# Expert tiles of 128 slots, two to a round, and another schedule for the last batch

## The chip, the cores and the metric

One core of a Trainium2 chip runs the whole program. The time is the device time of one execution in microseconds; what is compared is the median of several executions. The core's engines are TensorE (PE, with its weight loads listed as PEld), VectorE (DVE), ScalarE (ACT), GpSimd (POOL) and SyncE (SP), which issues nearly all transfers. Everything is in float32.

## The reference

The input is eight images of 256 channels and 32 x 32 pixels, so 1024 tokens of 256 numbers each. Two layers follow one another.

Layer 0 is a deformable attention: from a group norm of x come queries and sampling offsets; 64 keys and values per group are sampled; the scores get a bias that a small network of three layers computes for each pair of a pixel and a sampled point.

Layer 1 works on tokens:

```python
t = _to_tokens(x)
t = t + _L1_attn_ref(_ln_t(t), L1_attn_q_weight)   # sigmoid((t q) t^T) t
t = t + _L1_ffn_ref(_ln_t(t), L1_ffn_router_w, L1_ffn_w1, L1_ffn_b1, L1_ffn_w2, L1_ffn_b2)

# in _L1_ffn_ref: 8 experts, the best 2 for each token
probs = softmax(tokens @ router_w.T)
rw, re = top_k(probs, 2);  rw = rw / max(rw.sum(-1, keepdims=True), 1e-12)
combine = zeros((N, 8)).at[arange(N)[:, None], re].set(rw)
out = tokens
for e in range(8):
    h = gelu(tokens @ w1[e] + b1[e], approximate=False)
    out = out + combine[:, e:e + 1] * (h @ w2[e] + b2[e])
```

Each token needs two of the eight experts only, so a batch (one image) has 2048 pairs of a token and an expert.

## The kernel before

The eight batches run one behind another, and several stages of different batches are interleaved by Python generators, so that the order written in the program is the order on each engine's queue. A batch has 64 turns. Each turn does two of the 128 steps of the bias network: `first_layer` (L444: on POOL or DVE), `rectify` (ACT), `second_layer` (L462: matmuls `h2p`, then ACT or DVE), and every second turn `third_layer` (L480: matmuls `sim`). These matmuls are there in every turn. At every eighth turn `terms` (L413) loads two tables (`ta`, `nb`), which are used from three turns later on. Beside this a turn advances:

- `side`: the preparation of the next batch (`prep`, L227) and the softmax of this one;
- `mains`: the layer-1 attention. `attention` (L585) makes two generators. `upper` runs from turn 53 of a batch. `rest` begins at turn 0 of the next batch and goes on for some 55 turns: the last softmax, `to_query` (matmuls `wp`, `bp`, `q`), `slots` (twelve slots of matmuls `ap`, a sigmoid, matmuls `vp`), `finish` (layer norm, `un`, logits `lq`), then `route`, then 16 scatters;
- `mixtures`: the experts (`experts`, L867), one step where `mix` (L1038) says that one is due;
- `sums`: `combine` (L937), which gathers the results of a token's two experts (16 gathers on POOL), weighs and adds them and writes the output, one of 22 steps a turn.

`route` (L780) picks two experts for each token, counts the tokens of each expert, and gives every pair a slot. Slots are arranged in tiles that belong to one expert each. A tile has 256 slots; in the worst case 15 tiles are needed, and 15 are always computed. Row counts per expert are compared with the multiples of 256 in a constant of 8 x 8 x 4 numbers, from which come the first tile of each expert (`ends`), each pair's row (`slot`) and the expert of each tile (`expert`). POOL scatters the tokens to these rows of `xs` in device memory, with 16 indirect transfers of 128 rows.

`experts` is a pipeline of three stages over the tiles. In iteration n it multiplies tile n-2 by its second weight (`yp`, four matmuls), adds the bias on DVE (`yt`, L901) and writes `ys`; it issues the rows `xl` of tile n+2 and both weights of tile n+1, the latter behind one register load that fetches the expert's number; it multiplies tile n-1 by its first weight (`hp`, four matmuls of 256 columns) with a gelu on ACT (`ht`, L922); and it transposes tile n (`tp`, then the copy `xg`). Weight tiles have three buffers each. That is 19 steps: two that only load, and n from 0 to 16.

```python
        if of == b - 2 and b < NB - 1:
            due = i in (24, 26) or i > 26 and i % 2 and i not in (35, 37, 39, 61, 63)
        elif of == b - 3:
            due = i in (3, 7, 9)
```

So the experts of batch b-2 stand in 16 turns of batch b, and their last three steps in batch b+1. In batch 7 the second form of the rule holds: batch 5's experts follow batch 4's in turns above 9 that are odd or divisible by three, and batch 6's get turns 62 and 63. What is left stands behind the last turn, in a loop over `rest` of batch 7 (L1105): a step at every second advance outside the attention, and at every advance from the routing on. When the scatters of batch 7 have been issued, its experts run alone, interleaved with batch 6's `combine`, and then batch 7's `combine`.

SyncE works its queue in order: a transfer that waits for its data holds up those behind it.

Of the kernel before, what the change touches and what calls it, by code (L numbers as in the profile page):

```python
# [9 lines left out]
F32 = mybir.dt.float32  # L10
I32 = mybir.dt.int32
AF = mybir.ActivationFunctionType
ALU = mybir.AluOpType
# [14 lines left out]
SLOTS = 256  # L28
TILES = (2 * N + E * (SLOTS - 1)) // SLOTS
# [9 lines left out]
    ("ident", 128), ("gavg", 128), ("base", 512), ("basef", 128),  # L39
    ("gq", 1), ("cx", 1), ("cy", 8), ("rev", 64),  # L40
    ("ones", 128), ("before", 128), ("full", 256), ("tiles", (E - 1) * TILES), ("form", 12),
# [53 lines left out]
def tile_conv_attn_hybrid(ctx: ExitStack, tc: tile.TileContext, x, par, qw, w1, w2_, cst, out):  # L95
# [9 lines left out]
    wpool = ctx.enter_context(tc.tile_pool(name="w", bufs=3))  # L105
# [105 lines left out]
    xss = [nc.dram_tensor(f"xs{n}", [TILES * SLOTS, C], F32, kind="Internal").ap() for n in range(2)]  # L211
# [15 lines left out]
    def prep(b, xb, st):  # L227
# [41 lines left out]
        for t in range(KS * KS):  # L269
# [9 lines left out]
        oa = one.tile([P, 2, NJ], F32, name="oa")  # L279
        nc.scalar.activation(  # L280
            oa.rearrange("p k (y x) -> p k y x", x=8), oc.rearrange("p (y k) x -> p k y x", k=2), AF.Gelu
        )
# [4 lines left out]
        for g in range(2):  # L287
            for c in range(2):
                nc.tensor.matmul(
                    op.rearrange("p (c k g j) -> p c k g j", c=2, k=2, g=2)[:, c, :, g, :],  # L290
                    lhsT=pw[:, 2 * g + c : 2 * g + c + 1].to_broadcast([P, P]), rhs=oa, start=True, stop=True,
                )
        opf = psum("opf")
        nc.tensor.matmul(
            opf[:, 0:128].rearrange("p (k j) -> p k j", k=2),
# [6 lines left out]
        nc.vector.scalar_tensor_tensor(gk[:, 0:512], gk[:, 0:512], 4.0, base, ALU.mult, ALU.add)  # L302
# [7 lines left out]
        fl = one.tile([P, 2 * NJ], F32, name="fl")  # L310
# [9 lines left out]
        fr = one.tile([P, 2, 64], F32, name="fr")  # L320
# [22 lines left out]
        hx = one.tile([P, 256], F32, name="hx")  # L343
# [238 lines left out]
    def attention(b, st, o, rt):  # L582
# [152 lines left out]
        def rest():  # L735
# [10 lines left out]
            for n, _ in enumerate(slots([(q, mp) for q in range(4) for mp in range(2 if q < 2 else 0, 4)], True)):  # L746
                if n % 3 == 0:
                    yield
                    others()
# [7 lines left out]
            yield from route(lqs, rt)  # L757
# [3 lines left out]
            for n in range(16):  # L761
# [9 lines left out]
                yield  # L771
# [8 lines left out]
    def route(lqs, rt):  # L780
# [6 lines left out]
        revv = rev.rearrange("p (m e) -> p m e", e=E)  # L787
# [14 lines left out]
        def pick(name):  # L802
# [28 lines left out]
        nc.tensor.matmul(cnt, lhsT=cst_("ones"), rhs=sums, start=False, stop=True, skip_group_check=True)  # L831
        need = one.tile([P, E, E, 4], F32, name="need")
        nc.vector.tensor_tensor(
            need, cnt[:, 8, :].unsqueeze(1).unsqueeze(3).to_broadcast([P, E, E, 4]),
            cst_("full").rearrange("p (e f n) -> p e f n", e=E, f=E), ALU.is_gt,
        )
        nc.vector.tensor_reduce(ends[:, 1:9], need.rearrange("p e f n -> p e (f n)"), AX.X, ALU.add)
        for c in range(2):
# [4 lines left out]
            at, ends[:, 0:8].unsqueeze(1).to_broadcast([P, 8, E]), float(SLOTS), cnt[:, 0:8, :], ALU.mult, ALU.add  # L843
        )
        place = one.tile([P, 2, 8], F32, name="place")
        for c, oh in enumerate((oh1, oh2)):
# [5 lines left out]
        which = one.tile([P, TILES, E - 1], F32, name="which")  # L852
        nc.vector.tensor_tensor(
            which, ends[:, 1:8].unsqueeze(1).to_broadcast([P, TILES, E - 1]),
            cst_("tiles").rearrange("p (t e) -> p t e", e=E - 1), ALU.is_le,
# [11 lines left out]
    def experts(b, rt):  # L867
        xs = rt["xs"]
        yv = dram.tile([TILES * SLOTS, C], F32, name="ys")
        tiles = {}  # L870

        def fetch(t):
            xl = low("xl")
            nc.sync.dma_start(out=xl, in_=xs[t * SLOTS : (t + 1) * SLOTS, :].rearrange("(s p) c -> p s c", p=P))  # L874
            tiles[t] = [None, None, xl]

        def weights(t):
            e = nc.sync.value_load(rt["expert"][0:1, t : t + 1], min_val=0, max_val=E - 1)
            f1 = wpool.tile([P, 2 * C + 2], F32, name="w1")
            nc.sync.dma_start(out=f1, in_=w1[bass.ds(e, 1)].rearrange("e p c -> (e p) c"))  # L880
            f2 = wpool.tile([P, 3 * C], F32, name="w2")
# [347 lines left out]
```

## Time and profile before

| | us |
|---|---|
| time, median of 3 runs | 3216.83 (3212.77 to 3220.61) |
| the profiled execution | 3218.55, of which 3216.8 is the span of its instructions |
| before the first turn | 72.9 |
| turns of batch 0, 1, 2 | 277.9, 337.4, 367.6 |
| turns of batches 3 to 6 | 376.0, 378.9, 375.1, 379.2 |
| turns 0 to 62 of batch 7 | 392.4 |
| last turn and last `rest` up to the end of its queries | 46.4 |
| last attention | 44.6 |
| end of the attention, routing | 30.1 |
| last scatters, up to the first rows of batch 7's experts | 31.4 |
| batch 7's experts | 75.1 |
| batch 7's sums | 31.8 |

A turn is told in the trace by its first `h2p` matmul: each turn has 16 records of them (the trace shows two records for each float32 matmul). Within a run of matmuls the time from one start to the next is the price; the listed durations overlap. Times are in microseconds from the first instruction.

### The profile page before, as it was taken

The page shows a single profiled execution, that of the slowest core. Times are in us where ns is not written, and L with a number is a line of the kernel's source. Part 1 is how long each engine was busy: PE and PEld are TensorE (multiplying, and loading weights), DVE is VectorE, ACT ScalarE, POOL GpSimd, SP SyncE. Part 2 cuts the span into 40 slices and gives each one's busy share as a digit, 9 for nine tenths or more (in the row PEclk, how much of TensorE's full clock was granted, in tenths as well). Part 3 has the DMA queues.
Part 4 walks back from the last instruction along what each step waited for, and adds up shares of the span by engine and source line. Part 5 has one row for each costly group of instructions (what it writes and reads, how often), then busy time and mean ns, then how long its engine had stood idle before and what let it go on. Part 6 is the DMA issues. An engine that isn't in the chain of part 4 may idle for free. (4 is left out here: it accounts for less than half of the span.)

```text
span 3216.8 us, 50328 instructions
## 1 busy us (share of the span) xinstructions
PE 2928.8 (91%) x19468; PEld 1465.1 (46%) x19468; DVE 2173.7 (68%) x2996; ACT 1841.1 (57%) x2435; POOL 1547.5 (48%) x945
## 2 busy tenths in 40 slices
PE   3888998899999998999989999999999999988986
PEld 2223343334545454554535445354544546523765
DVE  4898678967785787756876587757777464586122
ACT  3666565656566556655566566655566566545322
POOL 2546344744464454634555365543646343364123
PEclk7999999999999999999999999999999999999998
DMA  3311101210344123432335224441234333532277
GB/s 100 89 32 45 21 19 27 69 29 19 85 122 129 32 65 98 136 91 50 87 88 145 55 61 103 117 133 33 66 90 141 81 84 97 147 96 64 66 248 235
DMA packets 421567, 281.20 MB, mean 87 GB/s; under 512 B 283088, under 2 KB 378064, under 8 KB 421328
## 3 DMA queue, kind: packets, MB, share of 16 engines
q1 hardware_dynamic: 408752, 242.80, 28.4%
q0 software_dynamic: 12288, 33.57, 3.4%
q8 instruction: 153, 2.51, 0.3%
q10 hardware_dynamic: 288, 1.62, 0.1%
q14 instruction: 86, 0.70, 0.1%
HBM read 204.51 MB, written 73.40 MB: 86 GB/s over the span
## 5 line engine op out<-in xcount | busy, mean ns | idle before, releaser
L453 POOL TENSOR_TENSOR h<-ta,nb 128x1024 f32<-128x1024 f32 x512 | 1060.7, 2073 | 1122.9 <-PE h2p L466 1052.8
L466 PE MATMUL h2p<-h,pr__97 64*64 64x512 f32 x8192 | 1026.8, 611 | 118.8 <-DVE h L474 86.8
L474 DVE TENSOR_TENSOR h<-h2p,nc 128x1024 f32<-128x1024 f32 x512 | 624.2, 1219 | 518.0 <-PE h2p L466 512.4
L472 ACT ACTIVATE h<-h2p,pr__97 128x1024 f32<-128x1024 f32 x512 | 569.7, 1113 | 516.0 <-PE h2p L466 514.9
L451 DVE TENSOR_TENSOR h<-ta,nb 128x1024 f32<-128x1024 f32 x512 | 765.3, 1495 | 0.7 <-ACT ta L427 0.5
L458 ACT ACTIVATE h<-h 128x1024 f32<-128x1024 f32 x512 | 536.8, 1049 | 82.8 <-POOL h L453 82.7
L466 PEld LDWEIGHTS h2p<-h,pr__97 64*64 64x64 f32 x8192 | 256.1, 133 | 639.9 <-issue 303.6
L493 PE MATMUL sim<-h,pr__97 128*32 128x512 f32 x4096 | 506.5, 613 | 0.0
L493 PEld LDWEIGHTS sim<-h,pr__97 128*32 128x32 f32 x4096 | 108.6, 111 | 375.4 <-issue 375.4
L896 PE MATMUL yp<-w,ht 128*128 128x256 f32 x960 | 241.8, 396 | 18.7 <-ACT tn L630 10.7
L701 PE MATMUL ap<-qt,tn 128*128 128x256 f32 x1024 | 250.5, 388 | 0.5 <-ACT nc L439 0.5
L715 PE MATMUL vp<-tt,sg 128*128 128x256 f32 x1024 | 243.3, 381 | 0.3 <-ACT sg L706 0.3
L922 ACT ACTIVATE ht<-hp,w 128x256 f32<-128x256 f32 x240 | 100.8, 471 | 239.9 <-PE hp L916 200.6
L916 PE MATMUL hp<-xg,w 128*128 128x256 f32 x960 | 229.4, 382 | 6.0 <-ACT gk L299 2.8
L965 POOL DMA_INDIRECT gs<-ys,slot x128 | 139.1, 1087 | 193.2 <-DMA ys<-yt 57.8
L701 PEld LDWEIGHTS ap<-qt,tn 128*128 128x128 f32 x1024 | 185.2, 190 | 88.5 <-issue 55.9
L896 PEld LDWEIGHTS yp<-w,ht 128*128 128x128 f32 x960 | 178.8, 195 | 85.1 <-issue 31.8
L715 PEld LDWEIGHTS vp<-tt,sg 128*128 128x128 f32 x1024 | 193.2, 190 | 33.2 <-issue 6.9
L901 DVE TENSOR_TENSOR yt<-yp,w 128x512 f32<-128x512 f32 x120 | 82.6, 688 | 176.6 <-PE yp L896 137.9
L916 PEld LDWEIGHTS hp<-xg,w 128*128 128x128 f32 x960 | 183.0, 191 | 33.3 <-ACT gk L299 3.7
L763 POOL DMA_INDIRECT xs<-ut,slot x128 | 166.9, 1304 | 47.9 <-DVE slot L850 26.2
L276 DVE SCALAR_TENSOR_TENSOR oc<-qp,pr__97,oc 128x128 f32<-128x128 f32 x280 | 168.7, 603 | 7.2
(264 smaller groups left out, 2550.6 us busy)
## 6 DMA issues: line engine op xcount, KB each, us to landing
w<-in_w SPq DMA_DIRECT2D x120, 384.0 KB, 3.9
ta<-fd SPq DMA_DIRECT2D x128, 256.0 KB, 5.5
w<-in_w SPq DMA_DIRECT2D x120, 257.0 KB, 3.2
xl<-xs SPq DMA_DIRECT2D x120, 256.0 KB, 3.0
ys<-yt SPq DMA_DIRECT2D x120, 256.0 KB, 2.3
nb<-fd SPq DMA_DIRECT2D x128, 128.0 KB, 5.2
xb<-in_x SPq DMA_DIRECT2D x8, 1024.0 KB, 7.9
x<-in_x SPq DMA_DIRECT2D x8, 1024.0 KB, 8.5
```

Of the source, the lines that this page charges most:

```text
L276: nc.vector.scalar_tensor_tensor(oc, tap, dw[:, t : t + 1], oc, ALU.mult, ALU.add)
L451: nc.vector.tensor_tensor(h1, a, b, ALU.max)
L453: nc.gpsimd.tensor_tensor(h1, a, b, ALU.subtract)
L458: nc.scalar.activation(h1, h1, AF.Relu)
L466: nc.tensor.matmul(h2p[gs, r, :], lhsT=par_("w2")[rs, gs], rhs=h1[rs, g].rearrange("p y x -> p (y x)"), start=True, stop=True, tile_positi ...
L472: nc.scalar.activation(h2, h2p, AF.Relu, bias=par_("cb2"))
L474: nc.vector.tensor_tensor(h2.rearrange("p r (y x) -> p r y x", x=W), h2p.rearrange("p r (y x) -> p r y x", x=W), nc_.unsqueeze(3).to_broad ...
L493: nc.tensor.matmul(sim[32 * q : 32 * q + 32, :], lhsT=par_("z3")[:, 15 - m : 47 - m], rhs=h2s[2 * u + q // 2][:, q % 2, :], start=False, s ...
L701: nc.tensor.matmul(ap[:, u, :], lhsT=tn[:, k, m0 : m0 + P], rhs=qt[:, k, quarter(q)], start=(k == 0), stop=(k == 1),)
L715: nc.tensor.matmul(vp[:, i, :], lhsT=sg_[:, u, i * P : (i + 1) * P], rhs=tt[:, 2 * mp + u, :], start=(first and u == 0 and i == 0), stop=( ...
L896: nc.tensor.matmul(yp[:, s, :], lhsT=ht[:, f, s * P : (s + 1) * P], rhs=f2[:, f * C : (f + 1) * C], start=(f == 0), stop=(f == 1),)
L916: nc.tensor.matmul(hp[:, f, :], lhsT=f1[:, k * C + f * P : k * C + (f + 1) * P], rhs=xg[:, k, :], start=(k == 0), stop=(k == 1),)
```

## The change

- Batches 0 to 6 have tiles of 128 slots. At most 23 are needed (24 with a spare), and two neighbouring tiles, which may belong to different experts, form a round. 12 rounds are always computed, each of 256 rows. Batch 7 keeps 15 tiles of 256.
- A round loads `xl` and writes `ys` as before. It loads two first and two second weights, each behind a register load of its own. `hp` has eight matmuls of 128 columns, gelu four calls; `yp`, `yt`, `tp` keep their shapes. An expert stage has 16 steps.
- The two weights have pools of their own with two buffers each, every buffer for two tiles. The second weight of round n is now loaded in iteration n (it is used in n+2), the first weight of round n+1 also in iteration n but behind that iteration's gelu. In batch 7's experts these places change too.
- `route` takes the tile size, counts the tiles of each expert first and sums them up in a second step; three small tiles now lie in PSUM.
- `prep` shares buffers (`oa`, `fl`, `fr`, `hx` lie in others), and one addition is split in two; constants shrink from 1599 to 767 columns.
- `mix`: in batches 2 to 6 the steps at turn 59 and at turns 3 and 7 of the next batch are gone. In batch 7 batch 4 has its last step in turn 1, batch 5 its 16 in turns 2 to 11, 24 to 26, 33, 35, 37 and 39, and batch 6 its first eight in the odd turns from 45 to 59.
- In batch 6's `rest`, which runs in batch 7's turns, the attention takes a slot in each turn (13 advances instead of 18), and two scatters go in a turn.
- Behind the last turn, a step of batch 6's experts stands at every fourth advance outside the attention instead of at every second; from the routing on at every advance, as before.

```diff
-                if n % 3 == 0:
+                if n % 3 == 0 and b != NB - 2:
                     yield
                     others()
...
-                yield
+                if n % 2 or b != NB - 2:
+                    yield
...
+        slots_ = LARGE if b == NB - 1 else SMALL
+        several = LARGE // slots_
+        rounds = -(-tiles_of(slots_) // several)
...
+        def weights(t, pool, width, w, name):
+            f = pool.tile([P, 2, width], F32, name=name)
+            for u in range(several):
+                n = t * several + u
+                e = nc.sync.value_load(rt["expert"][0:1, n : n + 1], min_val=0, max_val=E - 1)
+                nc.sync.dma_start(out=f[:, u, :], in_=w[bass.ds(e, 1)].rearrange("e p c -> (e p) c"))
+            return f
...
+            if n + 2 < rounds:
                 fetch(n + 2)
-            if n + 1 < TILES:
-                weights(n + 1)
+            if n < rounds:
+                second[n] = weights(n, w2pool, 3 * C, w2_, "w2")
...
                 for f in range(2):
-                    for k in range(2):
-                        nc.tensor.matmul(
-                            hp[:, f, :], lhsT=f1[:, k * C + f * P : k * C + (f + 1) * P], rhs=xg[:, k, :],
-                            start=(k == 0), stop=(k == 1),
-                        )
+                    for u in range(several):
+                        us = slice(u * slots_, (u + 1) * slots_)
+                        for k in range(2):
+                            nc.tensor.matmul(
+                                hp[:, f, us], lhsT=f1[:, u, k * C + f * P : k * C + (f + 1) * P], rhs=xg[:, k, us],
+                                start=(k == 0), stop=(k == 1),
+                            )
...
+            if n + 1 < rounds:
+                first[n + 1] = weights(n + 1, w1pool, 2 * C + 2, w1, "w1")
...
-        if of == b - 2 and b < NB - 1:
-            due = i in (24, 26) or i > 26 and i % 2 and i not in (35, 37, 39, 61, 63)
-        elif of == b - 3:
-            due = i in (3, 7, 9)
+        if b == NB - 1:
+            due = i in {
+                b - 3: (1,), b - 2: (2, 3, 4, 6, 7, 8, 9, 10, 11, 24, 25, 26, 33, 35, 37, 39),
+                b - 1: range(45, 60, 2),
+            }.get(of, ())
+        elif of == b - 2:
+            due = i in (24, 26) or i > 26 and i % 2 and i not in (35, 37, 39, 59, 61, 63)
         else:
-            due = b == NB - 1 and (i >= TURNS - 2 if of == b - 1 else of < b and i > 9 and (i % 2 or i % 3 == 0))
+            due = of == b - 3 and i == 9
...
-        if sorted_ or not attending and n % 2:
+        if sorted_ or not attending and n % 4 == 3:
             step(mixtures)
```

## The prediction

> **What bounds the kernel now.** I read the busy shares first, then the busy time by stage, with the 64 turns of a batch told apart by the starts of the second-layer matmuls (16 records a turn).
>
> ```profile
> PE 2928.8 (91%) x19468; PEld 1465.1 (46%) x19468; DVE 2173.7 (68%) x2996; ACT 1841.1 (57%) x2435; POOL 1547.5 (48%) x945
> ```
>
> PE is the likely bound, but a share is a mean; the stages say where. In the next fence the columns are the window, its length, each engine's busy time, the granted clock, the DMA share and GB/s. The rows: batch 1 (no expert work in its turns), batch 2 (16 steps of it), batch 3 (19, as in batches 4 to 6), batch 7 without its last turn; then, after the turns, the end of the last attention with the routing, the last scatters, the last batch's experts.
>
> ```profile
> 350.80:688.20 337.40, 304.15 (x2122) 127.15 (x2121) 264.28 (x342) 200.86 (x250) 181.70 (x101) 0.97 0.16 35
> 688.20:1055.80 367.60, 350.63 (x2375) 171.58 (x2374) 258.36 (x354) 223.92 (x294) 176.95 (x101) 0.99 0.29 79
> 1055.80:1431.80 376.00, 358.64 (x2434) 181.88 (x2433) 272.38 (x373) 229.30 (x304) 193.86 (x117) 1.00 0.35 90
> 2565.00:2957.40 392.40, 359.81 (x2377) 178.99 (x2377) 252.12 (x322) 229.64 (x289) 188.43 (x125) 0.98 0.36 98
> ...
> 3048.40:3078.50 30.10, 24.83 (x114) 18.93 (x113) 11.27 (x39) 8.71 (x18) 2.17 (x3) 0.94 0.54 173
> 3078.50:3109.90 31.40, 27.35 (x130) 22.13 (x129) 5.56 (x10) 8.74 (x20) 15.45 (x16) 1.00 0.77 257
> 3109.90:3185.00 75.10, 67.55 (x313) 55.43 (x313) 15.26 (x29) 21.37 (x48) 15.47 (x16) 0.93 0.88 289
> ```
>
> Batch 2 adds 46 us of PE work to batch 1 and only 30 us of time: a step of expert work partly fills turns in which PE waits. So a removed step isn't worth its PE time; it is worth what its turn is longer than the same turn without it. Batches 1 and 2 give that directly. Turns 59 and 60 of batch 1 (no step) and batch 5 (a step in turn 59):
>
> ```profile
> 658.51:671.46 12.95, 11.33 (x76) 4.03 (x72) 8.01 (x6) 10.10 (x15) 7.23 (x3) 1.00 0.16 32
> 2151.61:2169.09 17.48, 14.87 (x97) 7.40 (x93) 6.44 (x7) 10.12 (x17) 3.83 (x2) 1.00 0.48 138
> ```
>
> The instructions in order of time give the prices (start, us, engine, line; in brackets the idle time before and what ended it).
>
> ```profile
> 617.22 3.84 PE L374 MATMUL kv<-wt,xt 128*128 128x128 f32 x32
> 620.99 1.95 PE L466 MATMUL h2p<-h,pr__97 64*64 64x512 f32 x16
> ...
> 1401.14 3.60 PE L896 MATMUL yp<-w,ht 128*128 128x256 f32 x8 [2.14 <-ACT tn L630]
> ...
> 2982.62 1.89 PE L916 MATMUL hp<-xg,w 128*128 128x256 f32 x8
> 2984.35 0.60 PE L929 MATMUL tp<-cs,xl 128*128 128x128 f32 x4
> ...
> 3063.91 0.44 PE L795 MATMUL lp<-cs,lqs 128*128 128x128 f32 x2 [0.97 <-ACT xg L931]
> ...
> 3073.66 0.44 PE L830 MATMUL cnt<-run,cs 128*128 128x72 f32 x2 [0.54 <-ACT ht L922]
> ...
> 3078.55 1.03 POOL L763 DMA_INDIRECT xs<-ut,slot  x1 [24.21 <-DVE slot L850]
> ...
> 3097.61 0.96 POOL L763 DMA_INDIRECT xs<-ut,slot  x1 [0.30 <-issue]
> ...
> 3112.79 1.11 PE L929 MATMUL tp<-cs,xl 128*128 128x128 f32 x4 [4.42 <-DMA xl<-xs]
> ```
>
> Start to next start, today's hp group (four matmuls, 256 columns) takes 1.73 us; the 16 matmuls of kv, each with weights of its own and 128 columns, take 3.77, so 0.236 each. yp takes 1.73 (3101 to 3103), tp 0.44 (2994.30 to 2994.74). After an idle stretch PE runs at half speed: the yp at 1401 took 3.60. Last, the SyncE queue in one round, and the weights' time to landing while the last experts run:
>
> ```profile
> 3082.59 0.38 SPq L904 DMA_DIRECT2D ys<-yt  x1
> 3083.02 0.49 SPq L874 DMA_DIRECT2D xl<-xs  x1
> 3084.83 0.36 SPq L880 DMA_DIRECT2D w<-in_w  x1
> ```
>
> ```profile
> w<-in_w SPq DMA_DIRECT2D x15, 384.0 KB, 4.9
> ```
>
> **The change, part by part.**
>
> *A round.* Batches 0 to 6 have 12 rounds of two 128-slot tiles in place of 15 of one 256-slot tile. A round's yp and tp keep their shapes; hp becomes eight 128-column matmuls. By the kv row that is 8 x 0.236 = 1.89 us, +0.16. Here a rule speaks against the change: the Trainium skill (TensorE: Matmul & The Clock Gate, "Back-to-back issue gap") says that in a stream of weight load and matmul pairs N=128 sustains about 81 ns a matmul, where the isolated gap would be 56[...]. Scaled so, an estimate, hp would take 1.73 x 81/56 = 2.50 us, +0.77. The kv row is this shape, this type and fresh weights each time, so I take +0.16; by the rule 72 exposed rounds (12 in each of batches 2 to 7) would cost 55 us in place of 12. gelu has four 128-column calls for two of 256: 0.27 (a 128-column activation at 46.7 us) x 4 = 1.1 for 0.94; ACT is at 61% in batch 3, hidden behind PE, and 72 x 0.2 = 14 us if it weren't.
>
> *Batches 2 to 6.* The step in turn 59 goes. Turns 59 and 60 took 17.5, 19.1, 19.1, 17.5 and 19.2 us; without it 12.95 (batch 1): -27.6. Part of that is the slow yp at 1401, which stood behind a wait for tn. Turn 57 loses its tp: 5 x 0.44 = -2.2. In batches 3 to 6 the steps in turns 3 and 7 go; turns 3 to 8 took 34.3, and 33.6 in batches 1 and 2: 4 x 0.7 = -2.7. (The 7.5 us of PE work in those two steps filled waits of the softmax, so nearly nothing comes back.) hp: 5 x 12 x 0.16 = +9.6. Together -22.9.
>
> *Batch 7.* PE work is nearly the same: steps of batch 4 shrink to one, batch 5 has 3 fewer rounds, batch 6 gets eight steps (two fetch, one tp, five with hp, four with yp). But the rest of batch 6's attention has a slot in all of turns 12 to 24 in place of 18 turns, and expert steps stand elsewhere. I set each turn to its matmul work (the instructions in program order, each at its time from start to next start) where PE-bound turns of before do so (turn 14: 7.25 of work, 7.4 us), and to the measured length of a like turn where DVE or a wait bound it. Before and estimate: turns 0 to 11, 68.9 and 83.3 (nine steps move in); 12 to 26, 125.4 and 107.9; 27 to 34, 53.8 and 38.0 (no step in the routing); 35 to 42, 45.0 and 43.3; 43 to 53, 51.9 and 50.0; 54 to 62, 47.4 and 58.4. Sum -11.5. The moved scatters go two a turn: POOL then has 1.9 of first layer, 2 x 1.27, and from turn 40 a gather of 1.27, so 5.7 a turn for three turns; that is in the 43.3. The gathers of batches 4 and 5 move on POOL's queue to turns 1 to 16 and 39 to 54, one a turn.
>
> SyncE is the queue to watch. A round now issues ys, xl, two w2, two w1, each weight behind its own register load (1.3 us between xl's end at 3083.5 and w's start): 0.4 + 0.5 + 4 x 1.55 = 7.1 us for some 3.4. w1 also waits for this turn's gelu, because pools are two deep; queued behind it are the next ys, xl and every eighth turn the ta and nb loads (3.7 us), which aren't needed for three turns. In batches 2 to 6 rounds stand 10 us apart: hidden. In turns 6 to 11 of batch 7 they come every turn, at 7.4 us in the mean: SyncE just keeps up, with two turns of look-ahead. Bytes: 1.28 MB of weights and 0.52 MB of rows in 7.4 us are 245 GB/s, under the 289 of the last stage (and under the some 358 GB/s that the Trainium skill, DMA: Bandwidth & Descriptors, "Specifications", allows a core; the row is the stricter). Stalls: 0 to +12, I take +2. Batch 7: -9.5.
>
> *The tail.* From turn 63 to the last attention nothing is gained: three rounds stand before ov and q, and PE waits for the softmax and the statistics anyway. Then one round (not two) stands before the routing: the yp that ran at half speed (3.05), its hp and tp leave, about -5.2. Between lp and cnt two rounds remain (9.8 now, 9.3 after). So slot is ready 5.6 us earlier. Only two more rounds follow cnt, and PE is done long before the scatters. Today the first xl of the last batch sits on SyncE behind batch 6's ys writes until 3109.9, 12.3 after the last scatter began; then it waits only for the scatters' landing (3.5 in batch 4, 4.9 here), -7.5. Tail -13.1. With PE idle for 20 us the first matmuls run at half speed, as they do today (hp 3.75 at 3115.1).
>
> *The last batch's experts* keep 256-slot tiles, 4.33 us a round, PE-bound. But w2 is now fetched two rounds before its use instead of three, once yt has freed the buffer: yp 1.73 + yt 0.75 + SyncE 2.3 + landing 4.9 = 9.7 for two rounds, 4.85 a round. At the 3.7 of quiet stages it is 4.25, hidden. Between 0 and 13 x 0.5 = 6.5; w2 now issues ahead of w1 and not beside it, so I take +3.
>
> *The start.* The constants shrink from 1599 to 767 columns, 0.43 of the 2.9 MB that land by 9.8 us: -1.2 (0 to -2). The split of the offset addition, the smaller routing sums and the shared buffers are tenths of a microsecond a batch on DVE, beside PE work: 0.
>
> Sum: -22.9 - 9.5 - 13.1 + 3 - 1.2 = -43.7. The profiled execution took 3218.55 us (3216.8 of span); it stands 1.7 over the median of 3216.83. 3216.8 - 43.7 = 3173.
>
> **Rivals.**
> 1. PE-bound throughout: each batch shortens by all its removed PE work (batches 3 to 6 by 4.0 + 4.0 + 3.5 + 0.4 - 1.9 = 10.0 each, batch 2 by 2.5) and batch 7 packs like batch 3 (-17). 42.5 + 17 + 13 + 1 = -74: 3143. For it: 95% busy in batch 3. Against: turns 3 to 8, where 7.5 us of work was worth 0.7.
> 2. SyncE or weight landing binds where rounds are dense: +12 in batch 7, +6.5 in the last experts, some 5 in the routing's two rounds: -25, 3192. For it: 7.1 us of issues against 7.4 us turns. Against: the look-ahead.
> 3. hp runs at the pace of its weight loads (the rule above): +43 on the sum, -1, 3216: no change.
> 4. Slower: weight loads arrive late in every round of batches 2 to 7, because w1 waits for gelu with only two buffers. From 44 us over 72 rounds, 0.6 us a round, it decides; at 1 us it ends at 3245. Against: a round's cycle through w1 is about 7.1 + 4.5 + 0.75 over two rounds, 6.2 each, and most rounds are 10 apart; landing would have to pass 12 us.
>
> **How the numbers follow.** Forecast 0.63, rival 1 0.10, rival 2 0.19, rival 3 0.04, rival 4 0.04. A change of 0.2% (6.4 us) is about what can be told from none. Faster 0.93, same 0.03, slower 0.04. Range 3152 to 3194: rival 2's end above, part of the way to rival 1 below.
>
> **What would show it.** Right: turns 59 and 60 of batches 2 to 6 near 13 us; hp near 1.9 us; batch 7's turns near 383; the first xl of the last batch about 24 us after the slot cast; last experts' rounds between 4.3 and 4.8. Wrong: idle PE ended by w in front of hp or yp inside the turns, hp above 2.2 us, or turns 12 to 26 of batch 7 well over 108 us.

## The result, and the profile after

The changed kernel takes 3167.8 us (median, 3165.7 to 3178.94) beside 3215.3 us (3212.77 to 3220.61) for the kernel before: a ratio of 0.9857, 95% interval 0.9831 to 0.9884. The forecast was 3173 us. The profiled execution took 3165.7 us, of which 3163.9 is the span, 52.9 under the span before.

The share of the engines on the page of the changed kernel:

```profile
PE 2856.4 (90%) x19720; PEld 1419.7 (45%) x19720; DVE 2156.2 (68%) x2999; ACT 1807.9 (57%) x2522; POOL 1552.5 (49%) x945
```

PE lost 72 us of busy time, more than the span lost. The stages say what became of it. In the windows of the changed kernel (window, its length, busy time of PE, PEld, DVE, ACT and POOL with instructions, granted clock, DMA share, GB/s) the rows are batches 1, 2 and 3, the turns 0 to 62 of batch 7; then the end of the last attention with the routing, the last scatters up to the first `tp` of batch 7 (the row before the prediction ended 2.9 earlier, at the first `xl`), the last batch's experts:

```profile
347.05:689.39 342.34, 306.56 (x2118) 127.64 (x2117) 266.57 (x345) 200.87 (x250) 178.30 (x101) 0.97 0.16 35
689.39:1049.64 360.25, 344.91 (x2447) 171.57 (x2446) 257.90 (x356) 224.61 (x314) 177.04 (x101) 0.99 0.35 94
1049.64:1416.88 367.24, 350.33 (x2470) 175.12 (x2469) 270.83 (x373) 226.59 (x318) 194.85 (x117) 0.99 0.39 104
2518.15:2912.60 394.45, 362.37 (x2511) 185.34 (x2511) 233.64 (x323) 215.96 (x311) 192.92 (x125) 0.97 0.45 131
...
3003.34:3029.67 26.33, 20.93 (x125) 16.51 (x124) 10.59 (x40) 8.29 (x21) 2.16 (x4) 0.94 0.59 181
3029.67:3054.89 25.22, 2.50 (x13) 1.61 (x12) 1.45 (x4) 1.14 (x4) 19.27 (x20) 0.62 0.40 135
3054.89:3132.20 77.31, 66.40 (x313) 54.73 (x313) 15.18 (x28) 21.30 (x48) 11.60 (x12) 0.95 0.84 266
```

Against the rows before: batches 2 and 3 are 7.4 and 8.8 us shorter, batch 7's turns are no shorter at all, the scatters' stage up to the first `tp` took 25.2 instead of 34.2 and PE is nearly empty in it, and the last experts got longer. Term by term (stage lengths of the two profiled executions, in us):

| stage | before | after | moved | forecast |
|---|---|---|---|---|
| before the first turn | 72.9 | 69.7 | -3.2 | -1.2 |
| batches 0 and 1 | 615.2 | 619.7 | +4.4 | 0 |
| batches 2 to 6: turns 59, 60 | 92.3 | 57.2 | -35.2 | -27.6 |
| turns 57, 58 | | | -1.9 | -2.2 |
| turns 3 to 8 | | | -9.1 | -2.7 |
| turns 9 to 11 | | | -4.7 | 0 |
| everything else in them, hp among it | | | +2.9 | +9.6 |
| batch 7, turns 0 to 62 | 392.4 | 394.5 | +2.1 | -9.5 |
| tail, the last experts not counted | 187.5 | 174.0 | -13.5 | -13.1 |
| last batch's experts | 71.9 | 77.3 | +5.4 | +3.0 |
| sum | 3216.8 | 3163.9 | -52.9 | -43.7 |

(The last experts are counted from their first `tp` on, so the 71.9 is less than the 75.1 shown before the prediction. Turns 57 to 60 and 3 to 11 are summed over the five batches.) The sum came out near the forecast because batches 2 to 6 gave twice what was expected (48.0 us for 22.9) and batch 7's turns nothing. The experiments below take these two apart.

### The profile page after: what moved, and what is told of

It reads as the page before. It is cut to its first block, busy times and chain, and to the rows that moved or that the text cites. A ratio compares the mean times of both kernels' runs of the same rounds, so it can differ in the third digit from the quotient of the medians.

```text
span 3163.9 us, 51861 instructions
## 1 busy us (share of the span) xinstructions
PE 2856.4 (90%) x19720; PEld 1419.7 (45%) x19720; DVE 2156.2 (68%) x2999; ACT 1807.9 (57%) x2522; POOL 1552.5 (49%) x945
## 5 line engine op out<-in xcount | busy, mean ns | idle before, releaser
L505 PE MATMUL sim<-h,pr__100 128*32 128x512 f32 x4096 | 517.7, 625 | 0.0
L948 ACT ACTIVATE ht<-hp,w 128x128 f32<-128x128 f32 (+1 forms) x366 | 108.4, 376 | 210.1 <-PE hp L940 180.6
L922 PE MATMUL yp<-w,ht 128*128 128x256 f32 x792 | 195.6, 390 | 12.8 <-DMA w<-in_w 5.3
L940 PE MATMUL hp<-xg,w 128*128 128x128 f32 (+1 forms) x1464 | 195.9, 287 | 7.6 <-DMA w<-in_w 3.1
L922 PEld LDWEIGHTS yp<-w,ht 128*128 128x128 f32 x792 | 144.8, 191 | 73.4 <-issue 36.8
L927 DVE TENSOR_TENSOR yt<-yp,w 128x512 f32<-128x512 f32 x99 | 68.2, 689 | 150.9 <-PE yp L922 138.9
```

The lines of the kernel that those rows point to most:

```text
L505: nc.tensor.matmul(sim[32 * q : 32 * q + 32, :], lhsT=par_("z3")[:, 15 - m : 47 - m], rhs=h2s[2 * u + q // 2][:, q % 2, :], start=False, s ...
L922: nc.tensor.matmul(yp[:, s, :], lhsT=ht[:, f, s * P : (s + 1) * P], rhs=f2[:, s * several // 2, f * C : (f + 1) * C], start=(f == 0), stop ...
L940: nc.tensor.matmul(hp[:, f, us], lhsT=f1[:, u, k * C + f * P : k * C + (f + 1) * P], rhs=xg[:, k, us], start=(k == 0), stop=(k == 1),)
```

## The experiments

Runs on three chips. On each chip the kernel before was run beside the others: 3220.78 us (chip of the first four experiments), 3217.17 (the next four), 3231.01 (the last three). The changed kernel itself gave ratios of 0.9857 and 0.9812 in two sessions, so ratios of different sessions are not compared below 0.5%; what is smaller is read from the stages of the profiled executions.

### The tiles alone, and the schedule alone

First the small tiles with the old order of batch 7. The rules of the kernel before for batch 7 are put back; turns 59, 3 and 7 stay without a step.

```diff
-        if b == NB - 1:
-            due = i in {
-                b - 3: (1,), b - 2: (2, 3, 4, 6, 7, 8, 9, 10, 11, 24, 25, 26, 33, 35, 37, 39),
-                b - 1: range(45, 60, 2),
-            }.get(of, ())
-        elif of == b - 2:
-            due = i in (24, 26) or i > 26 and i % 2 and i not in (35, 37, 39, 59, 61, 63)
-        else:
-            due = of == b - 3 and i == 9
+        if of == b - 2 and b < NB - 1:
+            due = i in (24, 26) or i > 26 and i % 2 and i not in (35, 37, 39, 59, 61, 63)
+        elif of == b - 3:
+            due = i == 9
+        else:
+            due = b == NB - 1 and (i >= TURNS - 2 if of == b - 1 else of < b and i > 9 and (i % 2 or i % 3 == 0))
...
-                if n % 3 == 0 and b != NB - 2:
+                if n % 3 == 0:
...
-                if n % 2 or b != NB - 2:
-                    yield
+                yield
...
-        if sorted_ or not attending and n % 4 == 3:
+        if sorted_ or not attending and n % 2:
```

> The changed kernel with the last batch's schedule of before: attention with its extra advances, one scatter a turn, steps in turns above 9 that are odd or divisible by three, batch 6's experts from turn 62, a step at every second advance in the tail. Theory 1 (the rounds carry the gain, the new schedule of the last batch carries none): batches 1 to 6 as in the changed kernel (-43 us), five steps of expert work fewer in batch 7's turns (about -15), the tail's three rounds fewer (-9), the start -3, the last experts +5: near 3150 us. Theory 2 (rounds and schedule both gain, as the prediction's terms have it): no tail gain of 13 and no gain in batch 7's turns, 3180 us or more.

Measured: 3160.81 us, ratio 0.9822 (0.9799 to 0.9845). So the whole gain is there without the new order of batch 7: it comes with the small tiles and the steps that they take out of batches 2 to 6. Batch 7's turns took 379.6 us (394.5 in the changed kernel), and the tail 259.2 (251.3).

Then the reverse: the kernel before, with its 256-slot tiles, and the new order of batch 7 (the same turns, three more of them for its 19 steps).

```diff
+        if b == NB - 1:
+            due = i in {
+                b - 3: (1, 2, 3),
+                b - 2: (4, 6, 7, 8, 9, 10, 11, 24, 25, 26, 27, 28, 30, 33, 35, 36, 37, 39, 41),
+                b - 1: range(45, 60, 2),
+            }.get(of, ())
...
-                if n % 3 == 0:
+                if n % 3 == 0 and b != NB - 2:
...
-                yield
+                if n % 2 or b != NB - 2:
+                    yield
...
-        if sorted_ or not attending and n % 2:
+        if sorted_ or not attending and n % 4 == 3:
```

> The kernel before (15 tiles of 256) with only the last batch's new schedule: a slot of attention in every turn, two scatters a turn, batch 4's last three steps in turns 1 to 3, batch 5's 19 in turns 4 to 41, batch 6's first eight in the odd turns from 45 to 59, every fourth advance in the tail. Theory 1 (the schedule carries no gain): six steps more in batch 7's turns, about +15, and as much off the tail: 3215 us within 8. Theory 2: 3200 us or less.

Measured: 3211.33 us (14 executions), ratio 0.9972 (0.9963 to 0.9981). A real gain, but a small one: batch 7's turns took 402.0 (+9.6), the tail 242.4 (-17.0). With 15 rounds left to do, eight fewer behind the turns shorten the tail a good deal. With 12 rounds less is to be had there, as the next view shows. The old order with small tiles: the last `yp` of batch 6 and the first `tp` of batch 7 on PE, with idle time before and what ended it; the second fence has the first scatter:

```profile
3036.61 2.07 PE L921 MATMUL yp<-w,ht 128*128 128x256 f32 x8 [1.69 <-DMA w<-in_w]
3043.27 0.86 PE L957 MATMUL tp<-cs,xl 128*128 128x128 f32 x4 [4.60 <-DMA xl<-xs]
```

```profile
3015.94 1.03 POOL L775 DMA_INDIRECT xs<-ut,slot  x1 [25.13 <-DVE slot L869]
```

From the first scatter to batch 7's first `tp` 27.3 us pass, 25.2 in the changed kernel: rounds that the changed kernel did in batch 7's turns run here beside the scatters, where PE has nothing else to do, and all but 2 us of them are hidden. Ahead of the first scatter the tail is 5.4 longer. So in this pair of profiles the new order pays 14.8 us in the turns for 7.9 in the tail. Whether it loses in the end is another matter, to which the last session returns.

### The place of one step

In batches 2 to 6 the change drops the step of turn 59 because there are three steps fewer. Was it the work of that step, or the place? The changed kernel with the step of turn 57 moved back to 59:

```diff
-            due = i in (24, 26) or i > 26 and i % 2 and i not in (35, 37, 39, 59, 61, 63)
+            due = i in (24, 26) or i > 26 and i % 2 and i not in (35, 37, 39, 57, 61, 63)
```

> The changed kernel, in batches 2 to 6 one step moved from turn 57 to turn 59; the work is the same. Theory 1 (what was gained at turn 59 is its place: the step there waits behind the copy of tn, PE falls idle and then runs at half speed): 6 to 8 us in each of five batches come back, less some 1.5 us that turns 57 and 58 lose, so +22 to +32 us, 3190 to 3200. Theory 2 (the gain is the removed work): within 5 us of the changed kernel's 3168.

And the kernel before, all 15 tiles of 256, with its step of turn 59 moved to 35:

```diff
-            due = i in (24, 26) or i > 26 and i % 2 and i not in (35, 37, 39, 61, 63)
+            due = i in (24, 26) or i > 26 and i % 2 and i not in (37, 39, 59, 61, 63)
```

> The kernel before, in batches 2 to 6 one step moved from turn 59 to turn 35, in the middle of the routing; the work is the same. Theory 1 (turn 59 is a bad place whatever the tile size): turns 59 and 60 lose 6 us in each of five batches, and turn 35 takes 3 more: -15 us, 3200. Theory 2 (the gain needs the removed work): 3215 within 5.

Measured: 3182.95 us for the first, 0.9882 (0.9861 to 0.9903); its span is 20.6 over that of the changed kernel. 3194.87 us for the second, 0.992 (0.9895 to 0.9946); its span is 25.6 under the kernel before. One row of windows each, turns 59 and 60 of batch 5: the changed kernel; the step of 57 put in 59; the old tiles with the step of 59 put in 35.

```profile
2119.98:2131.41 11.43, 10.71 (x77) 3.95 (x73) 6.09 (x6) 8.59 (x14) 4.29 (x2) 1.00 0.27 73
```

```profile
2133.36:2152.53 19.17, 16.37 (x100) 8.69 (x96) 9.04 (x8) 10.34 (x18) 6.49 (x3) 0.91 0.34 91
```

```profile
2138.87:2150.30 11.43, 10.71 (x76) 3.96 (x73) 6.09 (x6) 8.59 (x14) 4.28 (x2) 1.00 0.45 133
```

Without the step the two turns take the same 11.43 with either tile. With it they take 7.7 more, with 5.7 more of busy PE time. The run with the step put in 59 shows why; PE in order of time, then two rows of ACT:

```profile
2133.36 2.23 PE L478 MATMUL h2p<-h,pr__100 64*64 64x512 f32 x16
2135.52 1.09 PE L639 MATMUL bp<-cs,tt 128*128 128x128 f32 x8
2138.89 2.58 PE L922 MATMUL yp<-w,ht 128*128 128x256 f32 x8 [2.28 <-ACT tn L642]
2141.27 3.05 PE L940 MATMUL hp<-xg,w 128*128 128x128 f32 x16
```

```profile
2137.14 1.24 ACT L439 ACTIVATE ta<-ta,pr__100 128x1024 f32<-128x1024 f32 x1
2138.27 1.05 ACT L642 COPY tn<-bp 128x512 f32<-128x512 f32 x2
```

`yp` reads `w` and `ht`, neither of which comes from `tn`. What it lacks is a place for its result. All matmuls whose results go to `psum(...)`, among them `bp`, `q`, `yp` and `hp`, share two buffers:

```python
    ps_m = ctx.enter_context(tc.tile_pool(name="ps_m", bufs=2, space=PSUM))
...
    def psum(name):
        return ps_m.tile([P, 512], F32, tag="ps", name=name)
```

The two halves of `bp` fill both, and a buffer comes free when ACT has copied it to `tn`. ACT first does a rectify and `ta`; its first copy ends at 2138.84, and `yp` starts at 2138.89, while the second copy is still running. So `yp` waits 2.28 us for a buffer. (That it is the buffer follows from the code and from these times; no run gave the pool a third one.) Then `hp`, partly at half speed, takes 3.05 where its listed duration is else 1.95. Without the step PE goes from `bp` straight to the next turn's `h2p`, whose buffers are of another pool, and that work covers the copy. Summed over the five batches, turns 59 and 60 moved by +37.0 and turns 57 and 58 by -15.7 in the first run; in the second turns 59 and 60 by -35.2, and turns 35 to 40, where the step went, by +13.3. So a step costs 7 us in turn 59 and 3 in the other two places. The move alone, with the tiles as they were, brings 25.6 of the 52.9 us by which the change shortened the span; 21.9 of them lie in the turns named, the rest in stages that also vary between runs.

### What makes batch 7's turns long

Turns of batch 7 by stretch, in us (estimate: the prediction's):

| turns | before | estimate | after |
|---|---|---|---|
| 0 to 11 | 68.9 | 83.3 | 90.0 |
| 12 to 26 | 125.2 | 107.9 | 108.4 |
| 27 to 34 | 53.8 | 38.0 | 39.1 |
| 35 to 42 | 45.1 | 43.3 | 39.8 |
| 43 to 53 | 51.9 | 50.0 | 61.0 |
| 54 to 62 | 47.5 | 58.4 | 56.2 |

The attention's stretch, 12 to 26, is as estimated to half a microsecond. Two stretches miss: 0 to 11 by 6.7 and 43 to 53 by 11.0. (Runs with the same instructions in them took 87.5 to 90.0 and 58.0 to 61.0, so some 3 us of either is spread.) Three causes were tried: the second pair of weight loads on SyncE, the scatters two at a time on POOL, the attention in every turn.

The changed kernel with one weight per round in place of two (the second tile of a round then uses the first one's expert):

```diff
-            for u in range(several):
+            for u in range(1):
...
-                            rhs=f2[:, s * several // 2, f * C : (f + 1) * C], start=(f == 0), stop=(f == 1),
+                            rhs=f2[:, 0, f * C : (f + 1) * C], start=(f == 0), stop=(f == 1),
...
-                                hp[:, f, us], lhsT=f1[:, u, k * C + f * P : k * C + (f + 1) * P], rhs=xg[:, k, us],
+                                hp[:, f, us], lhsT=f1[:, 0, k * C + f * P : k * C + (f + 1) * P], rhs=xg[:, k, us],
```

> The changed kernel, in batches 0 to 6 a round loads the weights of its first tile only and uses them for both tiles (the second tile's own weights are left out): half the weight traffic and half the register loads, 3.1 us less of SyncE a round. Theory 1 (SyncE's issues and the landing of the weights are hidden behind PE everywhere but in a few dense turns): 0 to -4 us against the changed kernel's 3168. Theory 2 (the second pair of weights is what kept batch 7's turns from getting shorter): -10 us or more, the gain in turns 0 to 11 and 43 to 62 of batch 7.

Measured: 3163.24 us, 0.9824 (0.98 to 0.9848). Turns 0 to 11 took 86.2 instead of 90.0, turns 43 to 53 took 59.6 instead of 61.0, the rest differs by 2.0 or less. Of the two, the first is 1.4 under the spread just given and the second inside it. The weights are not what is missing. PE's waits for `w` inside all turns of the changed kernel come to 0.4 us.

One scatter a turn, and batch 6's expert steps three fewer in the turns, since the routing's end comes later:

```diff
-                if n % 2 or b != NB - 2:
-                    yield
+                yield
...
-                b - 1: range(45, 60, 2),
+                b - 1: range(51, 60, 2),
```

> The changed kernel with one scatter a turn in batch 7 (turns 35 to 50), and batch 6's experts from turn 51, so five steps of them in the turns instead of eight and three more in the tail. Theory 1 (two scatters and a gather a turn make POOL the bound in turns 40 to 45, first-layer tiles come late and PE falls idle): turns 40 to 48 lose 5 us and more, the tail gets up to 10 longer where its three steps stand in front of the routing; 3168 to 3176. Theory 2 (the pairs cost nothing): the turns stay as they are and the time rises by the tail's 10.

Measured: 3158.05 us, 0.9804 (0.9776 to 0.9832). Batch 7's turns took 382.9 (-11.6), its tail 256.5 (+5.2). The turns gained in 43 to 53, 55.0 instead of 61.0, and 54 to 62, 50.6 instead of 56.2. In the second of these the steps are now earlier ones of the pipeline, with less in them. In the first it is the scatters: all of the 6.0 us lies in turns 43 to 46, which hold no matmul of an expert in either run. In turns 47 to 53 some 6.7 us of matmuls (three `tp`, two `hp`, one `yp`) are gone and six scatters have come; these turns took 37.9 instead of 37.1. Turns 43 to 46, first of the changed kernel, then with one scatter a turn:

```profile
2795.41:2819.25 23.84, 15.81 (x108) 3.76 (x105) 14.85 (x14) 11.05 (x12) 21.39 (x17) 0.79 0.43 149
```

```profile
2792.04:2809.10 17.06, 11.87 (x108) 3.10 (x105) 17.06 (x13) 9.89 (x11) 15.11 (x12) 1.00 0.20 62
```

The 108 records of PE are the same; POOL is busy for 21.4 of the 23.8 us. Its queue in the changed kernel:

```profile
2797.79 1.92 POOL L465 TENSOR_TENSOR h<-ta,nb 128x1024 f32<-128x1024 f32 x1
2799.88 0.99 POOL L775 DMA_INDIRECT xs<-ut,slot  x1 [0.17 <-issue]
2801.17 1.21 POOL L775 DMA_INDIRECT xs<-ut,slot  x1 [0.30 <-issue]
2802.68 0.98 POOL L993 DMA_INDIRECT gs<-ys,slot  x1 [0.30 <-issue]
2803.68 1.92 POOL L465 TENSOR_TENSOR h<-ta,nb 128x1024 f32<-128x1024 f32 x1
```

From one first layer to the next pass 5.9 us with two scatters and a gather, and some 4.4 in the run with one scatter. What ACT and PE wait for in turns 43 to 53 of the changed kernel (engine and line, releaser, us in all, times, longest), and what that looks like on PE:

```profile
ACT h L470 <- POOL h L465: 11.9, 5, 4.6
...
PE h2p L478 <- ACT h L484: 8.0, 3, 4.5
```

```profile
2801.85 3.69 PE L478 MATMUL h2p<-h,pr__100 64*64 64x512 f32 x16 [4.50 <-ACT h L484]
```

The first layer on POOL is late; ACT's `rectify` and then the second layer's matmuls follow it; and after 4.5 us without work the 16 records take 3.69 us instead of about 1.9. The other runs agree: in all thirteen profiles turns 43 to 46 hold no expert matmul, and they took 22.8 to 25.2 us in the eight with pairs of scatters and 17.1 to 19.4 in the five with one a turn. So pairs cost some 3 to 8 us where they meet the gathers, 6.8 in the two runs shown. In turns 35 to 42, mostly ahead of the gathers, they cost nothing: 39.8 in both runs. What single scatters would bring with all eight steps of batch 6 kept was not run.

The attention with the old gaps (no slot in every third advance, the scatters still two a turn; two expert steps fewer in the turns):

```diff
-                if n % 3 == 0 and b != NB - 2:
+                if n % 3 == 0:
...
-                b - 1: range(45, 60, 2),
+                b - 1: range(49, 60, 2),
```

> The changed kernel with the attention of batch 6 spread over 18 advances as before, so that the routing and the scatters come five turns later and batch 6's experts begin at turn 49 (six steps in the turns). Theory 1 (PE has the same work either way and is the bound in these turns): 3168 within 6. Theory 2 (a slot in every turn packs PE better): +8 us or more.

Measured: 3158.26 us, 0.9818 (0.9785 to 0.985). Batch 7's turns took 388.7. Running the attention without gaps is no gain with small tiles; nor, by its median, is it shown to be a loss.

### The last batch's weights

In the tail the second weight is fetched two rounds ahead instead of three. Here it is fetched three ahead again, two rounds to a buffer:

```diff
...
-            if n < rounds:
-                second[n] = weights(n, w2pool, 3 * C, w2_, "w2")
+            if several == 2 and n < rounds:
+                second[n] = weights(n, w2pool, 3 * C, w2_, "w2"), 0
+            elif several == 1:
+                for r in ((0, 1) if n == 0 else (n + 1,)):
+                    if r < rounds:
+                        if r % 2 == 0:
+                            pair[0] = w2pool.tile([P, 2, 3 * C], F32, name="w2")
+                        e = nc.sync.value_load(rt["expert"][0:1, r : r + 1], min_val=0, max_val=E - 1)
+                        nc.sync.dma_start(out=pair[0][:, r % 2, :], in_=w2_[bass.ds(e, 1)].rearrange("e p c -> (e p) c"))
+                        second[r] = pair[0], r % 2
```

> The changed kernel, in batch 7's experts the second weight is loaded three rounds before its use instead of two, in the free half of the same buffers. Theory 1 (the last experts wait for the second weight): the yp waits of 1.5, 0.9, 0.8 and 2.1 us go and the rounds come to 4.35 us: -5 us, 3163. Theory 2 (the transfers of that stage are the bound): no change, or the wait turns up in front of hp.

Measured: 3161.74 us, 0.9822 (0.9797 to 0.9847); the last experts' stage is 4.6 us shorter than in the changed kernel. (From the first `tp` to the end of the last `yp` it took 75.5 to 80.7 us in the seven profiles with small tiles and the weight two ahead, 72.9 to 74.9 in the three with the look-ahead.) In the changed kernel PE waits in this stage for weights in front of `yp`; with the look-ahead only `hp` still does. The two lists of waits, changed kernel and then look-ahead:

```profile
PE yp L922 <- DMA w<-in_w: 5.3, 4, 2.1
```

```profile
PE hp L948 <- DMA w<-in_w: 3.5, 4, 2.1
```

### Two combinations

On a third chip the changed kernel ran again, beside two combinations.

> The changed kernel itself, beside the two that follow, so that they are compared on one chip. Both theories: a ratio of 0.984 to 0.987 to the kernel before, 3165 to 3172 us.

Measured: 3170.45 us beside 3231.01, 0.9812 (0.9795 to 0.9829), 2.7 us from the first median, while the kernel before is 15.7 slower than in the first session.

The small tiles with the old order of batch 7 (the edit of the first experiment) and the look-ahead (the edit just shown):

> The rounds of two small tiles with the last batch's schedule of before, and in batch 7's experts the second weight three rounds ahead. Theory 1 (batch 6's 12 rounds already fit behind the last scatters, so that moving eight steps of them into the turns only lengthens the turns): 10 us under the changed kernel for the schedule and 4.5 for the look-ahead, 3150 to 3156, the fastest of all. Theory 2 (the earlier difference of the two schedules was between sessions): 3160 to 3166.

Measured: 3167.34 us, 0.9805 (0.9783 to 0.9828): not the 3150 to 3156 expected, and not to be told from the changed kernel. Batch 7's turns were short as before (381.3), but the tail took 268.6. There the rounds behind the last attention did not fit beside the scatters. Rows of SyncE, then of PE, the last one the first `tp` of batch 7:

```profile
3030.62 10.70 SPq L907 DMA_DIRECT2D w<-in_w  x4
...
3055.05 6.82 SPq L927 DMA_DIRECT2D ys<-yt  x2
3062.17 0.91 SPq L900 DMA_DIRECT2D xl<-xs  x2
...
3038.99 3.78 PE L921 MATMUL yp<-w,ht 128*128 128x256 f32 x8 [4.96 <-issue]
...
3065.01 1.11 PE L965 MATMUL tp<-cs,xl 128*128 128x128 f32 x4 [4.28 <-DMA xl<-xs]
```

Four weight loads take SyncE 10.7 us from first to last, and at the same time PE idles 4.96 us for nothing that the profile shows ("issue"). The rounds behind are late: `ys` waits 6.0 us for its `yt`, and the `xl` of batch 7, next on SyncE's queue, goes out only at 3062.17. That `tp` comes 38.7 us after the first scatter instead of the 27.3 of the other run in the old order. So what the rounds left beside the scatters cost differs between runs. Busy memory alone doesn't explain it: over the scatters 357 GB/s were moved in the other run and 259 in this one. Why the issues of both engines were so slow in this execution is open. Which of the two orders of batch 7 is the better one with small tiles is not shown.

Last, the look-ahead together with a schedule made from the stretches above: no steps of batch 5 in turns 10 and 11 (two of them go to 27 and 28), and batch 6's first eight partly in neighbouring turns rather than all in odd ones.

```diff
-                b - 3: (1,), b - 2: (2, 3, 4, 6, 7, 8, 9, 10, 11, 24, 25, 26, 33, 35, 37, 39),
-                b - 1: range(45, 60, 2),
+                b - 3: (1,), b - 2: (2, 3, 4, 6, 7, 8, 9, 24, 25, 26, 27, 28, 33, 35, 37, 39),
+                b - 1: (45, 46, 47, 51, 53, 55, 57, 58),
```

> The changed kernel with the look-ahead, and in batch 7 other turns for some steps: batch 5's from turns 10 and 11 to 27 and 28, batch 6's in 45, 46, 47, 51, 53, 55, 57 and 58 instead of the odd turns from 45 to 59. Theory 1 (steps at turns 10, 11 and 59 stand beside the copies of tn and qt, where PE falls idle): turns 0 to 11 lose 10 us and 27 to 34 gain 6, turns 54 to 62 lose 2: -6 us, and -4.5 for the look-ahead, 3156 to 3160. Theory 2 (the place doesn't matter there): 3162 to 3165.

Measured: 3159.53 us, 0.9783 (0.9763 to 0.9804), 10.9 us under the changed kernel's median on the same chip, and the best ratio there. Turns 0 to 11 in the changed kernel of that session, and in this one:

```profile
2518.09:2605.84 87.75, 79.79 (x558) 45.67 (x557) 50.78 (x68) 47.13 (x74) 35.36 (x24) 1.00 0.58 172
```

```profile
2519.48:2594.94 75.46, 71.09 (x502) 38.22 (x501) 52.27 (x65) 44.86 (x66) 39.09 (x26) 1.00 0.55 162
```

12.3 us less time for 8.7 less PE work; in turns 27 to 34, where the two steps went, 7.0 more for 8.0. In turns 10 and 11 of the changed kernel `yp` waits 2.1 us for ACT's `qt` and 0.7 for `tn`, and `q` waits 1.1 for a round's gelu: again matmuls that wait for one of the two buffers, as in turn 59. The last experts took 74.8 us instead of 78.7. The re-ordering of batch 6's steps brought nothing: turns 43 to 53 took 61.9 (the pairs of scatters are still there), 54 to 62 again 56.2.

## Why the prediction was right or wrong

The sum was right, 3173 us forecast and 3167.8 measured, and part of that is luck. In the two profiles batches 2 to 6 gave 25.1 us more than forecast; batch 7's turns (11.6), the last experts (2.4) and the first two batches (4.4) took 18.4 of that away.

*A round.* Right to take the kv row and not the rule. 16 records of `hp` with 128 columns take 1.78 us from start to the next start (the median of the changed kernel; the rows are from batch 5), where the row said 1.89 and the rule 2.50:

```profile
1980.30 1.95 PE L940 MATMUL hp<-xg,w 128*128 128x128 f32 x16
1982.09 0.60 PE L958 MATMUL tp<-cs,xl 128*128 128x128 f32 x4
```

The split costs 0.06 us a round where +0.16 was booked: over the 60 rounds of batches 2 to 6 some 3 us for 9.6, about the +2.9 in the table. Rival 3, which rests on the rule, falls with it.

*Batches 2 to 6.* The mechanism, a step is worth what its turn is longer, held: the drop of turn 59's step was the largest single gain, and the two experiments on its place show that it is the place that costs, with its wait for the copy of `bp`. Its size was under by 7.6, because the like turn that the step took from batch 1 (12.95) held 1.6 of idle PE time itself; in batches 2 to 6 the two turns now take 11.43. For the steps in turns 3 and 7 the forecast of 0.7 a batch was too small: turns 3 to 8 gave 9.1 and turns 9 to 11, not forecast at all, 4.7. Part of the 9.1 isn't the change's: batch 2 lost no step there and gained 1.7, and batches 3 and 4 of the changed kernel do the same work in these turns in different times:

```profile
1066.86:1100.49 33.63, 29.02 (x198) 10.99 (x195) 26.07 (x41) 15.75 (x18) 13.05 (x8) 0.90 0.14 25
1434.10:1466.12 32.02, 27.47 (x199) 10.80 (x195) 26.11 (x41) 15.75 (x18) 12.87 (x8) 0.95 0.15 25
```

The granted clock, 0.90 and 0.95, is the difference. The like turns from which the 0.7 came, 33.6 in batches 1 and 2, had the longer form. In the three profiles that keep the two steps turns 3 to 8 of batches 3 to 6 always take 34.2 to 34.3; in the ten without them 30.3 to 33.7. No run takes out these steps alone.

Rival 1 came nearer here than the forecast (42.5 for 48.0), but not by its reason. A step's own work is not its price: the one in turn 59 was worth 7.0 us a batch for 4.0 of matmuls, the two in turns 3 and 7 about 3 for 7.5.

*Batch 7.* Here the prediction is wrong by 11.6, and by its own sign (turns near 383): they took 394.5, and 390.5 to 393.0 in the three other profiles with the same turns. "I set each turn to its matmul work" was right for turns 12 to 34 and 54 to 62, where PE is the bound. Two steps failed. The first is the term of the moved scatters. The price was right, 5.7 us a turn forecast and 5.9 measured from one first layer to the next, but not the place: it was put into turns 35 to 42, while the last pairs ran on POOL at 2807.06, in turn 44. So turns 35 to 42 took 3.5 us less than estimated, 43 to 53 took 11.0 more, and after its waits PE ran at half speed, which the sum left out. How much of the 11.0 the steps from turn 47 on add is not separated. The second is turns 10 and 11, where the matmuls of rounds and queries wait for each other's buffers; taking the steps out there shortened turns 0 to 11 by 3.6 us more than PE's busy time.

The term named as the risk, SyncE, was mis-sized the other way: taking half of the weight loads away gave at most 5 us in the two stretches that missed, where 17.7 were missing, and PE's direct waits for `w` inside the turns are 0.4. (Its sums slip a little: a weight at 1.3 + 0.36 makes 7.5 us a round for 7.1, and the bytes by the tile sizes 248 GB/s for 245. The `yp` in the rows at 3102 takes 1.83, not 1.73. None of these decides anything.) So rival 2's +12 in batch 7 nearly came true, but for another reason; its cause holds for the last experts only. Rival 4, late weights in every round, is refuted by the same 0.4, and rival 1's -17 for batch 7 by its +2.1.

*The tail.* The routing came 4.1 us earlier where 5.6 was forecast, and the wait from the first scatter to the first `tp` fell by 9.0 where 7.5 was forecast. The first `xl` no longer waits behind `ys` writes (it goes out at 3051.27, 2.6 us after the last scatter began, where 12.3 passed before); PE now waits for the scatters alone:

```profile
3029.67 1.05 POOL L775 DMA_INDIRECT xs<-ut,slot  x1 [20.06 <-DVE slot L870]
...
3048.71 0.96 POOL L775 DMA_INDIRECT xs<-ut,slot  x1 [0.30 <-issue]
...
3054.89 1.08 PE L958 MATMUL tp<-cs,xl 128*128 128x128 f32 x4 [22.27 <-DMA xl<-xs]
```

Between the last scatter's start and the first `tp` 6.2 us are left, and PE had been idle for 22.27. Either part of the change brings most of the 9.0: with small tiles in the old order this stage took 27.3 (but 38.7 in the run with the look-ahead), with the old tiles in the new order 25.1. The runs point to the rounds that are left beside the scatters: with three more of them, in the run with one scatter a turn, it took 34.0.

*The last batch's experts.* Right mechanism, size off: +5.4 for +3. Waits of `yp` for `w` sum to 5.3, and the look-ahead took 4.6 back. Four rounds take 5.1 to 6.4 us, the others 4.3 to 4.9.

*The start and the rest.* -3.2 for -1.2, within what the start varies by between runs (69.7 to 72.9 in all profiles). Batch 1 has no expert step, but the changed routing and preparation run in it; they were booked at 0. It was 5.0 longer in this pair and 1.4 to 5.1 longer in the other runs of small tiles, against 1.3 and 1.6 in the two runs that keep the old tiles. Of the 5.0, 3.3 lie in turns 32 to 44, in part at a lower clock, and 1.75 in turn 54 at full clock. The cause is open.

## What to carry to other kernels

Ask where a step stands before asking what it costs: a step whose result needs a buffer that another chain still holds pays that wait, the half-speed stretch after it and its own work; moving one such step in each of five batches took 22 us out of the turns concerned, where the whole change brought 53. When small work is put into pairs, look at the queue that carries it and at what else stands there: two scatters and a gather between two first layers set POOL's pace, and through it PE's. A price that is right but in the wrong turns still spoils the estimate. Where several terms are uncertain in both directions, check each by its own stage after the run, for a sum that comes out right does not show that its terms are.

## What the runs showed of the hardware

- PE can fall to half speed after an idle time well under 3 us. The granted clock changes in steps of 3.41 us. The run with the step put in turn 59, around the 2.28 us in front of its `yp`:

```profile
2136.75:2140.16 3.41, 1.27 (x6) 1.14 (x7) 1.47 (x2) 2.57 (x4) 1.18 (x1) 1.00 0.02 5
2140.16:2143.57 3.41, 3.41 (x15) 3.14 (x14) 1.82 (x2) 0.00 (x0) 0.00 (x0) 0.50 0.12 42
```

  PE was busy for 1.27 of 3.41 us, and the next 3.41 ran at a clock of 0.50. The trace of the changed kernel has 859 such stretches at full clock. In the 32 that were followed by half speed PE was busy for at most 2.10 us, in the others for at least 1.52. The Trainium skill (TensorE: Matmul & The Clock Gate, "What's actually happening") puts the fall of the clock after at least one idle window of about 3.4 us that runs freely; the length agrees, but here a window need not be idle throughout.
- Equal turns differ by that clock: turn 4 of the changed kernel takes 6.86 us at 1.00 in batch 4 and 8.50 at 0.80 in batch 3, with the same instructions.
- Four weight loads took SyncE 10.7 us from first to last in one stage of the last scatters, and 3.04 (at 3049.03) a little later in the same run.
- The median of the kernel before lay between 3215 and 3231 us in four sessions, that of the changed one at 3168 and 3170 in two.
